# Unread constant products on TensorE ahead of its waits, in a two-layer attention and feed-forward kernel

## The chip, the core and the metric

One Trainium2 chip; the program runs on one of its cores. The metric is the device time of one execution in microseconds (us). Three runs of the kernel before took 1187.93, 1188.32 and 1190.07 us; the median is 1188.32 us.

## The reference

Two transformer layers over 2 batches of 1024 tokens with 256 features. Each layer adds an attention and a feed-forward part, both computed from the same layernorm of x:

```python
xn = _layernorm(x)
x = x + attn0(xn) + ffn0(xn)   # causal, 32 heads of 8 on 8 kv heads, rope; gelu ffn on values rounded to e4m3
xn = _layernorm(x)
x = x + attn1(xn) + ffn1(xn)   # see below
```

`attn1` regroups the tokens by position, with 16 heads of 16. `ffn1` rounds its weights to ternary values per group of 64, multiplies silu(gate) by up, normalises the rows by their root mean square and projects back.

## The kernel before

The tokens lie as 16 tiles `xs` of 128 rows. `xnT` holds the layernorm, transposed, in four chunks of 512 tokens.

**Layer 0** is `attention0`. `project` makes q and k, `split` cuts each into three bfloat16 parts (on VectorE for the first chunk, on GpSimd later), and `load_q` brings the parts back through DRAM into `qmain` and `qlast`. SyncE issues these DMAs in program order. For each of the 16 query tiles i (listed in `order`) there are two passes over the keys. `max_unit` (masks L887, scores L910, tile `m`) feeds the row maximum on VectorE (`mx`, L922); `take_max` and `turn_max` send the maxima through DRAM into `qlast` (L949, L951). `weigh` then makes the shifted scores (L974, tile `s`), ScalarE takes the exponential (L984, `p`), and `gather` multiplies by v (L1004, `acc`). `one_slot` interleaves three streams by counting: the maxima of later tiles (`advance`), the pieces of the layer-0 feed-forward (`ffn0`, tiles `gu`, `f0o`), and the ternary weights and second layernorm. A ternary piece is three steps of VectorE (L329, L331, L332) behind a product (`tpsg`, L327). `next_late` runs pieces of the layernorm of layer 1 for chunks whose sums are ready. `rest_of_weights` and `next_late` are each called from a slot. TensorE's instructions keep the order in which the code records them (`manual_schedule`); the order on VectorE, ScalarE, GpSimd and SyncE is made by a scheduler from estimated times.

PSUM pools in layer 0: `ps_s` (3 buffers, tiles `m` and projections), `ps_t` (4 buffers, nearly all else, `s` and `vp` among them), `ps_acc` (1).

**Layer 1** is `layer1`, whose order is a heap of functions keyed by due times: `at(delay, f)` puts f at `now + delay`. Unit 1.0 of that time is about one `ffn_unit` (`f1gu`, L627). For each chunk: `project` (`pqk` L435, `pv` L452), `turn` (`pt` L464, then a write `qkv` and loads of `qs`, `ks`, `vs` by SyncE, L467 and L469), `scores` (`sq` L484, maximum on VectorE L492, which goes through DRAM into `qs`, L494 and L497), `shifted` (`sk` L519 and the exponential L527), `weighted` (`acc` L534), `normalise` (`ot` L548, VectorE L550 and L552), `turn_back` (`ob` L564, `rows` L565). The last chunk ends in `attended_by_heads` (`ao` L592): 32 products for each of four token groups, 16 rows deep, whose sums VectorE adds to x (L596) before the output DMAs. `ffn_out` is `f1o` (L662).

Of the kernel before, what the change touches and what calls it, by code (L numbers as in the profile page):

```python
# [10 lines left out]
F32 = mybir.dt.float32  # L11
# [8 lines left out]
P = 128  # L20
# [28 lines left out]
def two_layers(ctx: ExitStack, tc: tile.TileContext, a: dict, out: bass.AP):  # L49
    nc = tc.nc  # L50
# [18 lines left out]
    ident_bf = cp.tile([P, P], BF, tag="ident_bf", name="ident_bf")  # L69
# [4 lines left out]
    for name, op, fill, sign in (  # L74
# [5 lines left out]
        for e in range(2):  # L80
            for t in range(2):
                part = m[HALF * e : HALF * e + HALF, t, :]
                nc.gpsimd.affine_select(
                    out=part,
# [8 lines left out]
    groups = cp.tile([P, P], BF, tag="groups", name="groups")  # L93
# [36 lines left out]
    wv1 = k0_flat[0][:, 1024:1536].rearrange("p (k n) -> p k n", k=2)  # L130
    wp = k0_flat[1].rearrange("p (c d) -> p c d", d=D)


    mark = [None]

# [254 lines left out]
    def layer1(w, wgu, wp, cs, sc):  # L390
# [8 lines left out]
        with ExitStack() as es:  # L399
            pool = es.enter_context(tc.tile_pool(name="l1", bufs=2))  # L400
            dram = es.enter_context(tc.tile_pool(name="l1d", bufs=2, space=bass.MemoryType.DRAM))
            ps_s = es.enter_context(tc.tile_pool(name="l1s", bufs=1, space=PSUM))
            ps_gu = es.enter_context(tc.tile_pool(name="l1gu", bufs=2, space=PSUM))
# [8 lines left out]
            for n in range(2):  # L412
                q, k, v = (pool.tile([P, NH, P], F32, tag=f"{x}{n}", name=f"{x}s{n}", bufs=1) for x in "qkv")
                nc.gpsimd.memset(v, 1.0)
                for s in range(4):
                    nc.sync.dma_start(
                        out=k[S * s + HD : S * s + HD + 9], in_=a["same"][0, :, None, :].to_broadcast([9, NH, P])
                    )
                    nc.sync.dma_start(
                        out=q[S * s + HD : S * s + HD + 8], in_=a["same"][1, 0:8, None, :].to_broadcast([8, NH, P])  # L420
# [8 lines left out]
            def project(c, i):  # L429

                x = [xnT[c][:, k, i * P : (i + 1) * P] for k in range(2)]
                nm = f"{c}{i}"
                pqk = ps_m.tile([P, 512], F32, tag="m", name=f"pqk{nm}")
                for k in range(2):
                    nc.tensor.matmul(pqk, x[k], wqk[:, k, :], start=(k == 0), stop=(k == 1))  # L435

                pairs = pqk.rearrange("p (h f e) -> p h f e", f=8, e=2)
                shape = [P, 2 * NH, 2, 8]
                qk = pool.tile(shape, F32, tag="qk", name=f"qk{nm}")
                qk2 = pool.tile(shape, F32, tag="qk2", name=f"qk2_{nm}", bufs=1)  # L440
                for to, e, tab in ((qk, 0, cs), (qk2, 1, sc)):
                    nc.vector.tensor_tensor(
                        to,
                        pairs[:, :, None, :, e].to_broadcast(shape),
                        tab[:, None, :, (4 * c + i) % 8, :].to_broadcast(shape),
                        ALU.mult,
                    )
                nc.gpsimd.tensor_tensor(qk, qk, qk2, ALU.add)
                pv = ps_m.tile([P, 2, P], F32, tag="m", name=f"pv{nm}")
                for u in range(2):  # L450
                    for k in range(2):
                        nc.tensor.matmul(  # L452
                            pv[:, u, :], wv[:, k, u * P : (u + 1) * P], x[k], start=(k == 0), stop=(k == 1)
                        )
                all_t = pool.tile([P, 6, P], F32, tag="all", name=f"all{nm}")
                nc.scalar.copy(all_t[:, 4:6], pv)
                at(0.5, lambda: turn(c, i, qk, all_t))
# [187 lines left out]
            def ffn_scale(n):  # L645
                ss = hidden[n][1]
                pss = ps_m.tile([P, 4], F32, tag="m", name=f"pss{n}")
                for i in range(4):
                    nc.tensor.matmul(pss[:, i : i + 1], ss[:, i * P : (i + 1) * P], ones, start=True, stop=True)
                ms = pool.tile([P, 4], F32, tag="ms", name=f"ms{n}")  # L650
                nc.vector.tensor_scalar(ms, pss, 1.0 / HID, None, ALU.mult)
                inv = rsqrt(pool, ms, 4, RMS_EPS, f"f1_{n}")

                times = (0.1, 0.5, 0.9, 1.3) if n != chunks[-1] else (1.7, 2.85, 3.7, 4.3)
                for i, t in enumerate(times):
                    at(t, lambda i=i: ffn_out(n, i, inv))
# [40 lines left out]
            def at(delay, f):  # L697
                heapq.heappush(queue, (now + delay, next(counter), f))

            counter = itertools.count()  # L700
            for p, c in enumerate(chunks):
                for i in range(4):
                    at(8.0 * (p - 1) + 2.0 * i - 0.4 if p else 0.9 * i - 5.0, lambda c=c, i=i: project(c, i))
                for b in range(4):
                    at(8.0 * p + 2.0 * b, lambda c=c, b=b: scores(c, b))
                for hc in range(NHC):
                    at(8.0 * p + hc - 4.7, lambda c=c, hc=hc: ffn_unit(c, hc))
                at(8.0 * p + 8 - 4.7 + 0.6, lambda c=c: ffn_scale(c))
# [4 lines left out]
            while queue:  # L713
                now, _, f = heapq.heappop(queue)
# [3 lines left out]
    def attention0(w, qlast, tables):  # L718
# [11 lines left out]
        with ExitStack() as es:  # L730
# [3 lines left out]
            ps_s = es.enter_context(tc.tile_pool(name="a0s", bufs=3, space=PSUM))  # L734
            ps_t = es.enter_context(tc.tile_pool(name="a0t", bufs=4, space=PSUM))
# [129 lines left out]
            slot = 0  # L865
# [13 lines left out]
            def add_mask(out, start, stop):  # L879


                for t in range(2):
                    lo = HALF * t
                    for e in range(2):
                        rows = slice(HALF * e, HALF * e + HALF)
                        rhs = mask_q[rows, t, None, lo:]
                        nc.tensor.matmul(  # L887
                            out[e][:, :, lo:],
                            ident_h[rows, t, :],
                            rhs.to_broadcast([HALF, out[e].shape[1], P - lo]),  # L890
                            start=start and t == 0,
                            stop=stop and t == 1,
                        )


            mx = {}
# [219 lines left out]
            }  # L1116
            ready = []
            late, self_end, added = [], object(), [0] * NT
            unit = next(units)
            next(unit)  # L1120

            def rest_of_weights(u):
                with tc.issue_after(reduced.ins):
                    next(u, None)

            def next_weights():

# [15 lines left out]
                        after(6, lambda c=chunks: late.append(layernorm(1, c, pool, ps_t, "t")))  # L1143

            def next_late():
                if next(late[0], self_end) is self_end:
                    late.pop(0)

# [3 lines left out]
            at = 0  # L1152
            credit = share = 0.0
            cost_left = sum(cost for _, cost, _ in maxima)
# [2 lines left out]
            done_at = {}  # L1157

            def advance():
                nonlocal at, credit, cost_left  # L1160
                n, cost, unit = maxima[at]
                ready.extend(extra.pop(n, ()))
                unit()
                if ready:
                    ready.pop(0)()
                at += 1
                credit -= cost
                cost_left -= cost
                if cost == 0:
                    done_at[n] = slot  # L1170
                    if n >= 3:
                        next_weights()

            def one_slot(weights):

                nonlocal credit, share, pairs_left, pieces_left
                rate = max(cost_left / max(pairs_left - TAIL, 1), 512.0) * (1.0 if weights else 1.5)
                credit = min(credit + rate, 2.0 * rate)
                while at < len(maxima) and credit > 0 and order[maxima[at][0]] in qst:
                    advance()  # L1180
                share += max(pieces_left, 0) / max(pairs_left - TAIL, 1)
                if share > 0:
                    share -= 1.0
                    with tc.issue_after(reduced.ins):
                        next(pieces, None)
                    pieces_left -= 1
                if late and slot % 3 == 0:
                    with tc.issue_after(reduced.ins):
                        next_late()
                pairs_left -= weights  # L1190
                tick()

            group, waiting = [], None
            for n, (b, i) in enumerate(order):
                if n and n + 3 < len(order):
                    load_q(*order[n + 3])
                while n not in done_at or slot < done_at[n] + (LEAD if n > 2 else SHORT):
                    one_slot(False)
                for G in range(2):
                    for j in range(i + 1):  # L1200
                        for u in range(2):
                            one_slot(True)
                            if u and waiting:
                                gather(*waiting)
                            group += weigh(b, i, 2 * G + u, j)
                        waiting = (b, i, G, j, group)
                        group = []
# [116 lines left out]
```

## Time and profile before

| what | value |
|---|---|
| profiled execution, device time | 1187.45 us |
| its span (first to last instruction) | 1185.7 us |
| mean granted TensorE clock | 0.921 of full |
| busy: TensorE, VectorE, ScalarE, GpSimd | 86%, 65%, 46%, 28% of the span |
| median of three runs | 1188.32 us |

Line numbers are those of the kernel before. In the slices of the page each digit is a fortieth of the span (29.6 us) in tenths; `PEclk` is the TensorE clock that was granted. In the timeline a row is: start, length, engine, line, operation, output and inputs with their sizes, count, and in brackets the idle time of the engine just before and what ended it. In the waits a row is: who waited, for whom, us in total, times, longest. In the table of stretches a row is: the stretch and its length, then busy us (and instructions) of TensorE products, TensorE weight loads, VectorE, ScalarE, GpSimd, then the granted clock, the DMA share and GB/s.

### The profile page before, as it was taken

What the parts mean: (1) busy time and instruction counts of PE and PEld (TensorE: products, weight loads), DVE (VectorE), ACT (ScalarE), POOL (GpSimd) and SP (SyncE); (2) the same over time, 40 slices, a digit from 0 to 9 for tenths busy, and PEclk for the clock granted to TensorE, in tenths of its full rate; (3) what the DMA queues carried; (4) which work ended last, traced back from release to release, by engine and by line L of the source; (5) the groups of instructions that cost most, each with busy time, mean ns of one, the idle gap of its engine ahead of it and who ended that gap; (6) DMA issues with size and microseconds to landing.
All of it is one profiled execution on the core that took longest, in us unless ns stands there. A gap on an engine that the chain in (4) does not pass through costs nothing.

```text
span 1185.7 us, 19115 instructions
## 1 busy us (share of the span) xinstructions
PE 1021.4 (86%) x7340; PEld 493.4 (42%) x7340; DVE 765.5 (65%) x1448; ACT 542.6 (46%) x981; POOL 336.0 (28%) x384
## 2 busy tenths in 40 slices
PE   5463897897988989897989998978999999999987
PEld 2231331232432222232323333334576676676676
DVE  6677988889688997789896889244323334333321
ACT  1112352673456747576767776732223323323320
POOL 2023223314244021412123326454213313312200
PEclk9586797997899989998999999999899999999986
DMA  6631001002101010100010110029331421521200
GB/s 193 154 105 37 23 1 43 17 21 61 34 14 41 1 27 19 36 1 17 11 27 3 26 27 5 3 27 136 52 48 28 93 52 28 91 46 28 46 11 18
DMA packets 78850, 48.98 MB, mean 41 GB/s; under 512 B 31816, under 2 KB 73800, under 8 KB 78760
## 3 DMA queue, kind: packets, MB, share of 16 engines
q1 hardware_dynamic: 75512, 43.32, 17.5%
q0 software_dynamic: 2960, 4.20, 1.7%
q8 instruction: 57, 0.93, 0.3%
q14 instruction: 33, 0.27, 0.1%
q10 hardware_dynamic: 288, 0.26, 0.1%
HBM read 34.12 MB, written 15.20 MB: 42 GB/s over the span
## 4 chain that ended last, share of the span: by engine, by line
PE 57%; DVE 26%; DMA 4%; ACT 4%; issue 4%; POOL 3%; SPq 2%; DVEq 0%; ACTq 0%; POOLq 0%
DVE mx L922 14%; PE f1gu L627 9%; PE acc L1004 8%; PE s L974 7%; PE f1o L662 5%; PE m L910 3%; PE sk L519 3%; PE sq L484 3%; PE pqk L435 2%; PE gu L283 2%; PE m L887 1%; PE acc L534 1%; ACT p L984 1%; PE ao L592 1%; PE ot L1019 1%
## 5 line engine op out<-in xcount | busy, mean ns | idle before, releaser
L922 DVE TENSOR_REDUCE mx<-m 128x1 f32<-128x512 f32 (+3 forms) x608 | 372.8, 654 | 89.2 <-PE m L910 51.4
L984 ACT ACTIVATE p<-s 128x512 f32<-128x512 f32 x576 | 306.8, 605 | 147.6 <-PE s L974 144.4
L1004 PE MATMUL acc<-p,v 128*9 128x512 f32 x1152 | 171.2, 619 | 1.8 <-ACT p L984 1.2
L910 PE MATMUL m<-k,qmain 64*128 64x512 bf16 (+3 forms) x384 | 93.6, 361 | 53.1 <-DVE mx L922 36.1
L988 POOL TENSOR_SCALAR_AFFINE_SELECT p<-p 128x512 f32<-128x512 f32 x128 | 84.3, 682 | 175.7 <-ACT p L984 175.4
L627 PE MATMUL f1gu<-xnT,wgu 128*128 128x512 f32 x256 | 118.4, 606 | 1.6 <-DVE wgu L1229 1.6
L910 PE MATMUL m<-kmain,qmain 64*128 64x512 bf16 (+3 forms) x384 | 83.1, 332 | 24.5 <-DVE mx L922 22.6
L910 PEld LDWEIGHTS <-qmain 64*128 64x128 bf16 x768 | 50.2, 99 | 88.4 <-issue 62.9
L641 POOL TENSOR_TENSOR sq<-h 128x512 f32<-128x512 f32 x28 | 29.1, 1039 | 182.3 <-DVE h L637 182.3
L887 PEld LDWEIGHTS <-ident_h 64*128 64x128 bf16 x832 | 45.0, 97 | 84.0 <-issue 60.9
L974 PE MATMUL s<-qlast,k 35*128 35x512 bf16 x288 | 65.3, 399 | 16.4 <-DMA qlast<-mscr 16.4
L887 PE MATMUL m<-mask_q,ident_h 64*128 64x128 bf16 (+3 forms) x832 | 74.2, 221 | 3.2 <-DVE mx L922 2.2
L974 PE MATMUL s<-qmain,k 64*128 64x512 bf16 x288 | 69.0, 401 | 8.8 <-DVE att L1027 3.0
L627 PEld LDWEIGHTS f1gu<-xnT,wgu 128*128 128x128 f32 x256 | 47.6, 196 | 51.2 <-issue 47.9
L974 PEld LDWEIGHTS <-k 64*128 64x128 bf16 (+1 forms) x576 | 21.3, 96 | 114.4 <-issue 105.9
L974 PE MATMUL s<-qmain,kmain 64*128 64x512 bf16 x288 | 64.0, 389 | 4.8 <-ACT p L984 2.2
L636 DVE SCALAR_TENSOR_TENSOR h<-h,f1gu 128x512 f32<-128x512 f32 x32 | 21.9, 686 | 65.6 <-ACT h L635 65.6
L662 PE MATMUL f1o<-k,h 128*128 128x256 f32 x256 | 61.7, 398 | 0.5 <-DVE on L552 0.4
L974 PE MATMUL s<-qlast,klast 35*128 35x512 bf16 x288 | 61.1, 386 | 0.0
L492 DVE TENSOR_REDUCE m<-sq 128x16 f32<-128x2048 f32 x16 | 36.7, 2292 | 34.6 <-PE sq L484 33.9
L662 PEld LDWEIGHTS f1o<-k,h 128*128 128x128 f32 x256 | 50.5, 200 | 9.7 <-issue 1.7
L635 ACT ACTIVATE h<-f1gu 128x512 f32<-128x512 f32 x32 | 19.1, 597 | 64.6 <-PE f1gu L627 64.6
(270 smaller groups left out, 1556.5 us busy)
## 6 DMA issues: line engine op xcount, KB each, us to landing
qmain<-qscr SPq DMA_DIRECT2D x64, 96.0 KB
qkv<-all SPq DMA_DIRECT2D x16, 384.0 KB
qscr<-ptq SPq DMA_DIRECT2D x32, 96.0 KB
x<-in_x SPq DMA_DIRECT2D x16, 128.0 KB
qmain<-qscr SPq DMA_DIRECT2D x32, 64.0 KB
qs<-qkv SPq DMA_DIRECT2D x16, 128.0 KB
ks<-qkv SPq DMA_DIRECT2D x16, 128.0 KB
vs<-qkv SPq DMA_DIRECT2D x16, 128.0 KB
```

Source lines behind the costliest of these rows:

```text
L484: nc.tensor.matmul(ps[:, s, r, :], columns(q, slice(S * s, S * s + HD + 8), 4 * b + r), columns(k, slice(S * s, S * s + HD + 8), 4 * b + r ...
L492: nc.vector.tensor_reduce(m, ps, AX.X, ALU.max, negate=True)
L519: nc.tensor.matmul(ps[:, s, r, :], columns(k, slice(S * s, S * s + HD + 9), 4 * b + r), columns(q, slice(S * s, S * s + HD + 9), 4 * b + r ...
L627: nc.tensor.matmul(ps[g], wgu[:, k, g * HID + hc * P : g * HID + (hc + 1) * P], xnT[n][:, k, :], start=(k == 0), stop=(k == 1),)
L662: nc.tensor.matmul(po, hs[hc // 2][:, hc % 2, i * P : (i + 1) * P], wp[:, hc, :], start=(hc == 0), stop=(hc == NHC - 1),)
L887: nc.tensor.matmul(out[e][:, :, lo:], ident_h[rows, t, :], rhs.to_broadcast([HALF, out[e].shape[1], P - lo]), start=start and t == 0, stop ...
L910: nc.tensor.matmul(sc[e][:, s * width : (s + 1) * width], qst[b, i][0][rows, p, :], kst[b][0][rows, p // 4, lo : lo + width], start=not fo ...
L922: reduced = nc.vector.tensor_reduce(mx[b, i][:, part, e, pairs[0] : pairs[0] + n], sc[e][:, : n * width].rearrange("p (s k) -> p s k", s=n ...
L974: nc.tensor.matmul(sc[e], kst[b][n][rows, u, j * P : (j + 1) * P], qst[b, i][n][rows, 4 * u : 4 * u + 4, :], start=n == 0, stop=n == 1,)
L984: nc.scalar.activation(p, sc[e], AF.Exp, scale=scale)
L988: nc.gpsimd.affine_select(out=by_head, in_=by_head, compare_op=ALU.is_ge, fill=0.0, base=0, pattern=[[0, 4], [1, P]], channel_multiplier=-1,)
L1004: nc.tensor.matmul(acc[32 * s : 32 * s + HD0 + 1, :], vst[b][:, j, 4 * G + s, :], ps[s], start=(j == 0), stop=(j == i),)
```

## The change

A helper issues n products of two constants (`groups` as stationary, the identity repeated four times as moving operand: 128 rows, 512 columns, bfloat16) into a PSUM tile that nobody reads. It is called in these places; nothing else is edited.

```diff
+    def keep_busy(out, n):
+        rhs = ident_bf[:, None, :].to_broadcast([P, 4, P])
+        for _ in range(n):
+            nc.tensor.matmul(out.rearrange("p (h q) -> p h q", h=4), groups, rhs, start=True, stop=True)
...
+            def busy_later(delay, pool_, n):
+                def f():
+                    tag = "gu" if pool_ is ps_gu else "s"
+                    shape = [P, 512] if pool_ is ps_gu else [P, 4, 512]
+                    t = pool_.tile(shape, F32, tag=tag, name=f"busy1_{next(counter)}")
+                    keep_busy(t if pool_ is ps_gu else t[:, 0], n)
+                at(delay, f)
...
+            for t, n in ((-4.51, 11), (-1.81, 7), (-0.01, 10)):
+                busy_later(t, ps_s, n)
+            for t, n in ((25.99, 8), (27.99, 8), (29.49, 5), (32.9, 4), (33.36, 4)):
+                busy_later(t, ps_gu, n)
...
+            def wait_busy(n):
+                if n:
+                    keep_busy(ps_t.tile([P, 512], F32, tag="t", name=f"busy{slot}_{n}"), n)
...
             def rest_of_weights(u):
+                nonlocal long_steps
                 with tc.issue_after(reduced.ins):
                     next(u, None)
+                long_steps += 5
...
             def next_late():
+                nonlocal long_steps
+                long_steps += 2
...
             def advance():
...
+                if at == 0:
+                    wait_busy(56)
+                wait_busy(long_steps)
+                long_steps = 0
                 unit()
...
+                if n == 0:
+                    wait_busy(50)
                 for G in range(2):
```

Counted in the built program, that is 247 products: 56 ahead of the first `max_unit`, 50 ahead of the first `weigh`, 84 in 24 blocks of layer 0 (60 behind the 12 ternary pieces, 24 behind 12 layernorm pieces; each ahead of the next `max_unit`, one ahead of a later `ao`), 28 in three blocks at the start of layer 1 and 29 in five blocks at its end. In layer 0 the tile of a block takes the next of the four `ps_t` buffers.

The scheduler reorders a few instructions of the other engines around this. Two of the moves are not neighbours' swaps. On VectorE, two maxima (`mx`, L922) and a conversion step (`wg`, L198 and L200) go from ahead of the layernorm statistics of chunks 2 and 3 (L160) to behind its reciprocal root. At the start of layer 1, the second pair of `qk` (L442) goes behind the four `xn` steps (L172) of the last layernorm, and on ScalarE the first copy `all` (L465) behind the square root (L145).

More of the change, by code (lines that the diff above doesn't have):

```diff
@@ L1159, in advance @@
             def advance():
-                nonlocal at, credit, cost_left
+                nonlocal at, credit, cost_left, long_steps
                 n, cost, unit = maxima[at]
                 ready.extend(extra.pop(n, ()))
+                if at == 0:
+                    wait_busy(56)
+                wait_busy(long_steps)
+                long_steps = 0
                 unit()
```

## The prediction

> **What bounds the kernel now.** I read the page's slices first, then its chain of waits, then TensorE's waits, then the table of stretches over every time at which the granted clock was 0.5.
>
> ```profile
> PE   5463897897988989897989998978999999999987
> DVE  6677988889688997789896889244323334333321
> PEclk9586797997899989998999999999899999999986
> ...
> PE 57%; DVE 26%; DMA 4%; ACT 4%; issue 4%; POOL 3%; SPq 2%; DVEq 0%; ACTq 0%; POOLq 0%
> ```
>
> TensorE holds 57% of the chain and VectorE 26%: in layer 0 (to 785 us) the two alternate, in layer 1 TensorE rules alone. The clock row is the point of the change: it dips where TensorE had waited. One product of exactly the added shape stands in the timeline, at both clocks:
>
> ```profile
> 230.23 1.89 PE L283 MATMUL gu<-xq,wg 128*128 128x512 bf16 x4
> ...
> 558.18 1.04 PE L283 MATMUL gu<-xq,wg 128*128 128x512 bf16 x4
> ```
>
> Four products, the last ending 0.61 and 0.39 us after its start, so one step costs (1.89-0.61)/3 = **0.427 us at half clock** and (1.04-0.39)/3 = **0.217 us at full**. Weight loads ran beside these. Nearest rows bound a step from both sides: a pair of 64-row products in 0.22 us (0.11 each) below, 0.427 above; I take 0.217 and 0.427.
>
> The stretches at half clock add up to 188 us from 21 us on, with TensorE busy for some 138 us of them. If all of that were TensorE-bound, half of it, 69 us, would be the price; most is not, because VectorE is the bound there.
>
> The Trainium skill (TensorE: Matmul & The Clock Gate, Part 1) says that the warm-up penalty is under 1% of a typical kernel's span and not worth modelling. By it the whole change could bring at most 12 us. The 138 us above don't bear that out as a limit, and no term below uses it.
>
> **Part 1, 56 products ahead of the first maxima.** TensorE idles 12.74 us from 32.8 to 45.5 for the q load. But the block's PSUM tile takes the buffer of the first `vp`, and the built program makes it wait for the first `v` addition (timeline):
>
> ```profile
> 37.10 0.61 DVE L860 TENSOR_TENSOR v<-vp,bv_bc 128x64 f32<-128x64 f32 x4
> ...
> 47.46 0.58 PE L910 MATMUL m<-k,qmain 64*128 64x128 bf16 x7 [1.71 <-DMA qlast<-qscr]
> ```
>
> So it starts at 37.3, when the clock has already fallen (35.0). The clock rose 4.2 and 3.1 us after dense work began at 10.4 and 21.7; the steps of the clock lie 3.41 us apart, so here at 41.9. 4.6 us at 0.427 are 10.8 products, the other 45.2 take 9.8 us: end 51.7. Masks and the first scores need 0.7, so the first maximum starts at 52.4 instead of 48.0: 4.4 late. Being warm gives back 3 x 0.4 (each unit of 1.9 us has 0.62 of VectorE waiting for TensorE), 0.9 (`lnt` 1.97 to 1.1) and 1.4 (`k01p` 5.0 to 3.64). **+1.0 us**; a rise at 3.1 or 6.8 us makes it +0.3 or +2.1.
>
> **Part 2, 50 products ahead of the first `weigh`.** TensorE waits there from 87.6 to 104.0, its longest wait:
>
> ```profile
> PE s L974 <- DMA qlast<-mscr: 16.4, 1, 16.4
> ```
>
> and in the table of stretches this one, at half clock throughout, is the longest:
>
> ```profile
> 79.40:110.10 30.70, 11.09 (x87) 6.06 (x89) 22.70 (x55) 6.07 (x11) 5.34 (x7) 0.50 0.11 28
> ```
>
> The block starts at about 86, runs cold to 89.6 (9 products) or 93.1 (16), and ends by 98.5 to 100.6: before the wait does. What sets that wait is not TensorE: ScalarE holds the cast of q (94.53) behind a square root (94.42) that needs eight statistics from VectorE (89.85 on), and SyncE holds `mscr` behind that q. The move on VectorE takes two maxima (0.55 each), 1.22 and 0.43 out from ahead of the statistics, less overlap: **-2.45 us**. It costs that these now wait for the block, where VectorE otherwise idles from 99 to 105. Then the work from 104.0 to 110.1 runs warm: `acc` 1.70 to 1.05 and three slots of scores by 0.4, partly covered by VectorE: **-1.5** (0 to -2.5).
>
> **Part 3, 24 blocks in layer 0, 84 x 0.217 = 18.2 us of TensorE.** From 170 to 760 us TensorE waits for the maxima and VectorE waits for scores about as much (TensorE's waits):
>
> ```profile
> PE m L910 <- DVE mx L922: 58.6, 93, 2.8
> ```
>
> I went through the timeline at each block. Free, since TensorE idles for VectorE just behind: at 175.0 (idle 2.60), 221.3 (2.10), 274.0 (1.23, for ScalarE), 476.8 (1.35), 531.9, 537.7, 560.6, 649.8 (1.03), 728.8. Paid in part: 348.5, 716.4 (0.5 each), 542.6 with 545.6 (0.3), 570.4 (0.2), 735.1 (0.3). Paid: 415.5 and 602.2 (1.1 each: VectorE was waiting for these scores), 684.2 (0.6), 525.3, 566.2, 740.9 and the one ahead of `ao` (0.43 each), 556.7 (0.3). Sum 6.6. What they save: the half-clock stretches at 229.6 (behind the idle 2.10; 1.0) and 550.4 (behind an idle of 2.81; VectorE waits 1.09 in it; 1.2). The long ones, from 181.8, 284.2 and 424.2, begin 5 to 10 us behind their blocks and stay. **+4.4 us**; ends -2.2 (all free) and +18.2 (nothing free, nothing saved). That most of a block lies on idle time is the row nearest to it, so I keep to the low half.
>
> **Part 4, the start of layer 1.** The blocks of 11, 7 and 10 take 2.4, 1.5 and 2.2 us in idle gaps of 2.57, 1.90 and 2.90. The first makes `pqk` 1.5 us faster, and that is worth nothing: SyncE issues the first `qkv` write only at 800.78, and DMA sets the pace to 830.5. The moved `qk` may delay the second tile by up to 1.0; I take 0, since it ends near where it was. The third block counts:
>
> ```profile
> 833.41 5.47 PE L627 MATMUL f1gu<-xnT,wgu 128*128 128x512 f32 x8
> ...
> 839.16 3.60 PE L627 MATMUL f1gu<-xnT,wgu 128*128 128x512 f32 x8
> ```
>
> 5.47 to 3.60 and `pt` 1.11 to 0.60: **-2.4 us**, and TensorE is the bound from there on.
>
> **Part 5, the end.** Two blocks of 8 (1.7 us) in idle gaps of 2.05 and 2.06 ahead of `sq`, where a half-clock window follows each:
>
> ```profile
> 1093.73 1.93 PE L534 MATMUL acc<-p,vts 128*32 128x128 f32 x32
> 1095.60 4.17 PE L627 MATMUL f1gu<-xnT,wgu 128*128 128x512 f32 x8
> ...
> 1160.24 1.08 PE L534 MATMUL acc<-p,vts 128*32 128x128 f32 x32
> ```
>
> 0.85 + 0.57 + 0.1 (`sq`) = 1.5 each: **-3.0**. The block of 5 (1.1) in the gap of 1.56 ahead of the `sk` at 1132.35: `sk` 3.3 to 2.1 and `f1o` 5.88 to 3.72: **-3.3**, if the window then passes. The two blocks of 4 (0.87 each) fill gaps of 0.81 and 0.68, at about +0.2, and `ao` starts warm:
>
> ```profile
> 1168.30:1171.70 3.40, 3.40 (x36) 2.98 (x32) 0.00 (x0) 0.00 (x0) 0.00 (x0) 0.50 0.00 0
> 1171.70:1175.10 3.40, 3.40 (x36) 2.97 (x32) 0.00 (x0) 0.00 (x0) 0.00 (x0) 0.50 0.00 0
> ```
>
> TensorE is busy throughout and the clock does not rise: products 16 rows deep don't lift it. So I expect it to fall after one warm window. `ao` is 32 steps of four, 0.427 cold (13.7 in all); one step warm, as for `f1o` of the same 256 columns, is 0.217. With 3.4 us warm instead of 0.75, 2.6 less, net **-2.4**; ends 0 and -5.8 (warm to its end). Behind `ao` only the additions and the output remain, so it comes off the time whole.
>
> The same page (table "Why this matters for your kernels") asks for no idle gap over about 3 us. Here the clock fell behind gaps of 1.56 and 2.05 us. By the page parts 4 and 5 would be worth nothing, and the sum would be 1189 us.
>
> **Sum:** +1.0 - 2.45 - 1.5 + 4.4 - 2.4 - 3.0 - 3.3 - 2.4 = -9.65. Against the profiled execution (1187.45; span 1185.7 and 1.75 around it) that is 1177.8; the median of the runs is 0.9 higher, so **1178.0 us**.
>
> **Rivals.** About 0.2% (2.4 us) can be told from no change.
> - *The layer-0 blocks hide wholly and `ao` stays warm*: part 3 -2.2, `ao` -5.8: 1187.45 - 19.65, **1168**. For: nine blocks lie on idle time already. Against: VectorE waits for scores at 415.5 and 602.2.
> - *The clock falls all the same*: a window that is half filled may count as idle (0.51 to 0.56 busy fell at 1130.7 and 130.6). Then part 1 +1.0, part 2 -2.45, part 3 +4.4, one block of 8 and the third of layer 1 -3.9: **1186.5**, no change.
> - *TensorE is the bound in layer 0* (the other side): the 84 products of part 3 fall on the path at 0.217 each, +18.2, where the rest brings -14.05: **1191.6**, slower. It decides once over 14 of the 18.2 us are paid. For: VectorE waits there for `m` as long as TensorE waits for it, and each block takes one of four `ps_t` buffers, so the next `weigh` may wait for an exponential. Against: 69 us of TensorE's time from 170 to 760 are idle (520.7 busy of 590).
>
> **Chances.** Forecast 0.52 (own range 1172 to 1184), first rival 0.20, second 0.12, third 0.16. Faster by over 0.2%: 0.72; within: 0.12; slower: 0.16. The range takes the first three, 1167 to 1189; most of the third is left out.
>
> **What would show it.** Part 1: first maximum later than 48.0 by about 4 us. Part 2: the first `s` of `qlast` near 102.5, full clock behind it. Part 3: idle of TensorE before `m` shrinking by 10 us or more; if VectorE's wait for `m` grows as much, the third rival. Part 4: no half clock ahead of 840. Part 5: `ao` in 10 to 11 us with its first part at 0.217. The forecast is wrong if the half-clock stretches from 830 on are still there, or if 170 to 760 us became longer by over 10 us.

## The result and the profile after

The changed kernel takes **1201.76 us** (median of 4 runs, 1199.76 to 1203.36) beside 1188.98 before: ratio 1.0111, 95% interval 1.0089 to 1.0133. It is slower by 13 us; 1178 was forecast. Its profiled execution has a span of 1200.8, 15.1 more than before.

The slices of the page after, and its chain:

```profile
PE   5777797997998989898989999989999999999998
...
PEclk8878897998997989999999999999999999999889
...
PE 62%; DVE 25%; ACT 4%; DMA 3%; POOL 2%; issue 2%; SPq 1%; DVEq 0%; ACTq 0%; POOLq 0%
```

The granted clock is higher (0.934 in the mean, 0.921 before; the second slice went from 5 to 8, the last from 6 to 9), and yet the time is longer: TensorE's share of the chain grew from 57% to 62%. So the change does to the clock what it says, and loses elsewhere.

Where: I matched TensorE's products of the two traces one by one. The lag is how much later a product starts than the same one before.

| stretch (us of before) | forecast | lag gained after |
|---|---|---|
| to the first `weigh`, 104 (56 and 50 products) | -1.45 | +1.9 |
| 104 to 124 | -1.5 | -0.3 |
| 124 to 773 (blocks of layer 0) | +4.4 | **+20.6** |
| 773 to 860 (start of layer 1) | -2.4 | -0.8 |
| 860 to 1090 | 0 | -3.1 |
| 1090 to 1118 (one block of 8) | -3.0 with the other 8 | -1.7 |
| 1118 to 1166 (the other 8, the 5) | -3.3 | +4.6 |
| `ao` to the end | -2.4 | -6.1 |
| sum | -9.65 | +15.1 |

The -3.1 lies where the change adds nothing; 2.5 of it is the clock: the half-clock stretch of before at 1018 to 1021 has none to answer it in this execution.

Both engines' waits, TensorE's first (changed kernel), then VectorE's (changed kernel, then before):

```profile
PE m L936 <- DVE mx L948: 55.0, 89, 2.6
...
PE s L1000 <- DMA qlast<-mscr: 2.4, 1, 2.4
```

```profile
DVE mx L948 <- PE m L936: 71.9, 49, 11.0
```

```profile
DVE mx L922 <- PE m L910: 51.4, 43, 6.1
```

The wait ahead of the first `weigh` went from 16.4 to 2.4, and the long stretch at half clock around it broke up (table of stretches, changed kernel):

```profile
83.40:93.70 10.30, 7.12 (x49) 3.84 (x49) 9.70 (x24) 0.00 (x0) 0.00 (x0) 0.50 0.15 41
93.70:107.30 13.60, 10.78 (x60) 4.81 (x59) 8.44 (x26) 3.60 (x6) 2.62 (x3) 1.00 0.14 34
107.30:114.10 6.80, 6.43 (x36) 2.00 (x37) 6.45 (x11) 2.75 (x7) 3.79 (x6) 0.50 0.03 7
```

But TensorE's wait for the maxima shrank only from 58.6 to 55.0, while VectorE's wait for scores grew by 20.5 (16.3 of it among the blocks, from 170 to 760 us of before; the rest at the first maximum). As the sign of its third rival the forecast had named a TensorE wait shorter by 10 us or more and a VectorE wait longer by as much; only the second half of that is here. From 173.4 to 782.2 (170 to 760 before) TensorE is busy 545.1 of 608.8 us (520.7 of 590): its idle time shrank by 5.6, its busy time grew by 24.4.

### The profile page after: what moved, and what is told of

The parts are those of the page before. It is cut to its first block, busy times and chain, and to the rows that moved or that the text cites. A ratio compares the mean times of both kernels' runs of the same rounds, so it can differ in the third digit from the quotient of the medians.

```text
span 1200.8 us, 19591 instructions
## 1 busy us (share of the span) xinstructions
PE 1073.8 (89%) x7571; PEld 507.9 (42%) x7587; DVE 762.4 (63%) x1448; ACT 544.9 (45%) x981; POOL 334.6 (28%) x384
## 4 chain that ended last, share of the span: by engine, by line
PE 62%; DVE 25%; ACT 4%; DMA 3%; POOL 2%; issue 2%; SPq 1%; DVEq 0%; ACTq 0%; POOLq 0%
DVE mx L948 14%; PE f1gu L634 9%; PE acc L1030 8%; PE s L1000 7%; PE f1o L669 5%; PE busy L139 4%; PE m L936 4%; PE sk L526 3%; PE sq L491 3%; PE gu L290 2%; PE pqk L442 2%; PE m L909 2%; ACT p L1010 2%; PE acc L541 1%; PE ao L609 1%
## 5 line engine op out<-in xcount | busy, mean ns | idle before, releaser
L936 PEld LDWEIGHTS <-qmain 64*128 64x128 bf16 x768 | 47.5, 98 | 82.6 <-issue 60.0
L909 PE MATMUL m<-mask_q,ident_h 64*128 64x128 bf16 (+3 forms) x832 | 71.5, 218 | 2.3 <-DVE mx L948 2.1
L139 PE MATMUL busy<-ident_bf,groups 128*128 128x512 bf16 x247 | 65.1, 409 | 7.8 <-DVE v L882 6.2
```

The source lines that it names most:

```text
L139: nc.tensor.matmul(out.rearrange("p (h q) -> p h q", h=4), groups, rhs, start=True, stop=True)
L909: nc.tensor.matmul(out[e][:, :, lo:], ident_h[rows, t, :], rhs.to_broadcast([HALF, out[e].shape[1], P - lo]), start=start and t == 0, stop ...
L936: nc.tensor.matmul(sc[e][:, s * width : (s + 1) * width], qst[b, i][0][rows, p, :], kst[b][0][rows, p // 4, lo : lo + width], start=not fo ...
```

## The experiments

All kernels below are the changed kernel with fewer or moved blocks. A diff with `-` lines is against it; one with `+` lines alone is against the kernel before, with the change's helpers left in. "ao" is the closing group of 16-row products, "layer 0" the start of layer 1's first product (`pqk`); both are from the one profiled execution, the rest from all runs. Ratios are to runs of the kernel before on the same chip (medians there 1187.8 to 1189.4).

| run | products kept | median us | ratio (95%) | layer 0 | ao |
|---|---|---|---|---|---|
| before | none | 1188.98 | | 784.9 | 13.4 |
| changed | all | 1201.76 | 1.0111 (1.0089 to 1.0133) | 807.1 | 7.2 |
| e1_blocks | layer-0 blocks | 1195.57 | 1.0062 (1.0038 to 1.0087) | 800.9 | 7.2 |
| e2_no_blocks | all but layer-0 blocks | 1185.36 | 0.9978 (0.9956 to 1.0) | 785.9 | 7.2 |
| e3_layer1 | eight blocks of layer 1 | 1182.42 | 0.9951 (0.9931 to 0.9972) | 788.3 | 7.2 |
| e4_ahead_weigh | the 50 | 1177.43 | 0.9905 (0.9872 to 0.9939) | 785.2 | 7.2 |
| s4_dense | 4 elsewhere | 1188.52 | 0.9998 (0.997 to 1.0027) | 785.2 | 7.2 |
| s10_dense | 10 elsewhere | 1188.21 | 1.0006 (0.9975 to 1.0037) | 789.2 | 13.3 |
| f24_single | layer-0 blocks of one | 1181.16 | 0.9949 (0.9926 to 0.9972) | 790.6 | 7.2 |
| f_one_at_348 | one layer-0 block | 1189.94 | 1.0017 (0.9991 to 1.0043) | 790.8 | 13.3 |
| h1_ao | 4 + 4 ahead of ao | 1182.34 | 0.9966 (0.9945 to 0.9987) | 788.1 | 7.2 |
| h2_weigh_ao | 50, 4 + 4 | 1175.07 | 0.9888 (0.9857 to 0.9918) | 785.4 | 7.2 |
| h3_blocks_ao | layer-0 blocks, 4 + 4 | 1195.38 | 1.0053 (1.0031 to 1.0075) | 804.5 | 7.2 |
| h4_first_ao | 56, 4 + 4 | 1180.33 | 0.9935 (0.9909 to 0.9961) | 787.9 | 7.2 |
| k1_without_two | layer-0 blocks but two, 4 + 4 | 1186.07 | 0.9979 (0.9961 to 0.9997) | 796.9 | 7.2 |
| k2_behind_scores | layer-0 blocks behind scores, 4 + 4 | 1186.45 | 0.9974 (0.9953 to 0.9996) | 796.7 | 7.2 |
| k3_first_weigh_ao | 56, 50, 4 + 4 | 1185.21 | 0.9947 (0.9928 to 0.9966) | 789.5 | 7.2 |
| k4_weigh_start_ao | 50, 11 + 7 + 10, 4 + 4 | 1176.37 | 0.9895 (0.9873 to 0.9917) | 787.0 | 7.2 |
| l1_27_weigh_ao | 27, 50, 4 + 4 | 1175.63 | 0.9903 (0.9866 to 0.9939) | 784.6 | 7.2 |
| k5_weigh_end | 50, 8 + 8 + 5 + 4 + 4 | 1179.69 | 0.9933 (0.9907 to 0.9959) | 784.9 | 7.2 |

One execution differs from the next by several us here: where the code of layer 0 is untouched, it ends between 784.9 and 789.2 in five traces.

### Which part loses: e1_blocks, e2_no_blocks, e3_layer1, e4_ahead_weigh

e1_blocks drops these lines:

```diff
-            for t, n in ((-4.51, 11), (-1.81, 7), (-0.01, 10)):
-            for t, n in ((25.99, 8), (27.99, 8), (29.49, 5), (32.9, 4), (33.36, 4)):
...
-                    wait_busy(56)
...
-                    wait_busy(50)
```

e2_no_blocks drops `wait_busy(long_steps)` alone, e3_layer1 all three `wait_busy` calls, and e4_ahead_weigh all but `wait_busy(50)`.

> Only the 24 blocks of layer 0 (84 products). The forecast's part 3 says +4.4, so 1193.4 beside 1189.0 before. Theory A (each product falls on the path: between 124 and 773 us the changed kernel's TensorE fell behind by 20.6 us): +18 to +23, 1207 to 1212. Theory B (the blocks hide and the changed kernel loses elsewhere): under +8.

> Everything but the 24 blocks of layer 0. The forecast's other parts say -14.05, 1175. Theory A with the lags read off the changed kernel's trace (+1.6 behind parts 1 and 2, about -7 over layer 1): 1183 to 1184, faster than before. Theory B (the loss isn't in the blocks): no faster than before.

> Only the eight blocks of layer 1. Forecast: -2.4 at the start and -8.7 at the end, 1178. By the lags of the changed kernel's trace: start -0.8, second block of 8 +3.9 (it landed ahead of a score product that waits for nothing), the rest of the end -9, about 1183. If the changed kernel's gains in layer 1 are only what a later start gives anyway: 1187 to 1189.

> Only the 50 products ahead of the first weighing. Forecast: -2.45 for VectorE's order and -1.5 for the clock, 1185. By the lag of the changed kernel (-2.2 at the first score of the weighing, -0.3 behind it): 1186.5. If what is won there is waited for again within layer 0 (VectorE's maxima set the pace): within 1 of before.

e1 fell just inside theory B's range (+7.4 us by the ratio, under 8 expected), e2 gained a mere 2.6, between its two theories, and e4 brought more than any of its expectations (-11.3). They don't add up: e1 and e2 make +5, the whole change +13. The traces say why e1 looks cheap. Its layer 0 ends 16.0 later than before's (800.9), and its layer 1, the same code as before, takes 392.9 where before's profiled execution took 400.7. Most of that is `ao`: 7.2 us at full clock in place of 13.4. So a warm `ao` is counted in e1 and in e2.

### Is it only where the clock's grid falls: s4_dense, s10_dense

```diff
+            for t, n in ((6.2, 4),):     # ((6.2, 10),) in s10_dense
+                busy_later(t, ps_gu, n)
```

No other block is kept.

> None of the change's blocks; instead 4 products (0.87 us) in the middle of layer 1's dense work at 874 us, where TensorE waits for nothing. In the profile of before the clock fell at 1018, 1093, 1110, 1154 and 1168 us; in that of the 50 products alone, with the same code in layer 1, not at 1018 and 1168. Theory C (which windows of 3.41 us are half empty is decided by where the work lies on the clock's grid, and the grid lies alike in most runs): a shift of 0.87 moves them, and the time falls by 3 to 8, to 1181 to 1186. If the grid lies differently in every run: +0.9.

> The same with 10 products (2.17 us). Theory C: a shift of 2.17 puts the work on the grid about where the run with the 50 products alone had it: faster than before by 3 to 9 although only work was added. If the grid lies differently in every run: +2.2, 1190.8.

Both are the same as before. Theory C falls. The clock changes only at points 3.41 us apart, its grid, and the grid starts anywhere: in the 20 traces the changes of the clock lie 0.2 to 3.4 us (modulo 3.41) behind the first product. What its place gives or takes is spread over the runs of one kernel (1179.1 to 1193.1 for s4) and doesn't shift the median. The Trainium skill (TensorE: Matmul & The Clock Gate, Part 1) says the same of the window, that it runs freely and one kernel differs by it from run to run; the traces agree.

### Products or places: f24_single, f_one_at_348

Both keep blocks of layer 0 alone, as e1_blocks does:

```diff
-                wait_busy(long_steps)
+                wait_busy(min(long_steps, 1))                                     # f24_single
+                keep_n += 1 if long_steps else 0                                  # f_one_at_348
+                wait_busy(long_steps if keep_n == 4 and long_steps else 0)        # f_one_at_348
```

> The 24 blocks of layer 0 with one product each (5.2 us in place of 18.2); the order on GpSimd changes in fewer places and no longer at 348 us. The 24 blocks alone cost 6.9. If their products' time counts: 6.9 x 5.2 / 18.2 = 2, 1190.6. If the place, the PSUM buffer and the order on the other engines count: +5 to +7. The forecast's working would give at most +1.

> Of the 24 blocks only the one at 348 us (5 products, 1.1 us), which alone puts two of GpSimd's additions of the feed-forward (x, L256) behind the last two steps of a ternary piece. The 24 blocks' trace falls behind by 4.9 there, that of the whole change by 6.8, with TensorE waiting 2.4 for ScalarE's cast and half clock for 13.7 us behind it. If that order is the cause: +4 to +7 at 380 us, and +3 to +7 on the time. If the product time is: +0.5 to +1.1.

f24_single came out 6 us faster than before, outside both expectations: its `ao` ran warm, and 11 of its 12 runs are below 1186. Why its `ao` starts warm so much oftener than before's is not shown. In layer 0 its trace lies 10.3 before that of e1, for 13.2 us of products less (61 at 0.217). f_one_at_348 can't be told from before by its time (+2.0, -1.1 to +5.1); its trace shows the mechanism. GpSimd (f_one_at_348, then before):

```profile
356.54 1.16 POOL L343 TENSOR_TENSOR wgu_bf<-tmg,twg 128x512 bf16<-128x512 bf16 x1
357.65 0.67 POOL L263 TENSOR_TENSOR x<-x,ob 128x256 f32<-128x256 f32 x1
358.27 0.59 POOL L328 DMA_DIRECT2D twg<-in_w_gate_up  x1
358.88 0.68 POOL L263 TENSOR_TENSOR x<-x,ob 128x256 f32<-128x256 f32 x1
```

```profile
354.05 0.67 POOL L256 TENSOR_TENSOR x<-x,ob 128x256 f32<-128x256 f32 x1
354.68 1.15 POOL L335 TENSOR_TENSOR tmg<-tmg,twg 128x512 bf16<-128x512 bf16 x1
355.79 0.67 POOL L256 TENSOR_TENSOR x<-x,ob 128x256 f32<-128x256 f32 x1
356.42 1.15 POOL L336 TENSOR_TENSOR wgu_bf<-tmg,twg 128x512 bf16<-128x512 bf16 x1
```

The same run's ScalarE and TensorE:

```profile
359.60 0.37 ACT L259 CAST ob<-f0o 128x256 bf16<-128x256 f32 x1 [3.85 <-POOL x L263]
```

```profile
360.31 0.37 PE L996 MATMUL s<-qmain,k 64*128 64x512 bf16 x1 [2.43 <-ACT ob L260]
```

The two additions now stand behind all four steps of the ternary piece. They hold the buffers of `ob`, so ScalarE's cast waits for them, the exponentials behind it wait too, and TensorE gets no free PSUM buffer for 2.43 us. Five unread products of 1.1 us moved an order on GpSimd, and its trace stands 3.5 behind at 360 us and 4.6 at 410, of which 1.1 were there ahead of the block. With one product there (f24_single) the additions keep their old places, and the lag stays at 1.3 across it.

### With ao made certain: h1_ao, h2_weigh_ao, h3_blocks_ao, h4_first_ao

To compare the other parts, all of these have the two blocks of 4:

```diff
+            for t, n in ((32.9, 4), (33.36, 4)):      # all four
...
+                    wait_busy(56)                     # h4_first_ao
+                wait_busy(long_steps)                 # h3_blocks_ao
...
+                    wait_busy(50)                     # h2_weigh_ao
```

> Only the two blocks of 4 around the last transpose, ahead of the closing ao. In the traces so far ao takes either 7.2 us (full clock to its end) or 13.3 to 13.4 (half), never between, and the runs of before cluster near 1181 and near 1189. Theory D (products 16 rows deep keep the clock they begin with, and before begins them at half clock in about four runs of five): all runs in the lower cluster, 1180 to 1186, median 5 below before. The forecast's term -2.4 (warm for one window only): 1186.5, with ao 10 to 11 us.

> The 50 products ahead of the first weighing and the two blocks of 4. With ao warm in both, this less the blocks of 4 alone is what the 50 are worth by themselves: by the trace of the 50 alone -1 to -3 at the end of layer 0. If that run's -11.2 was ao beginning warm by chance for the most: 1176 to 1180 here. If the 50 bring 11 by themselves: 1172.

> The 24 blocks of layer 0 and the two blocks of 4. Theory A (the products of the blocks fall on the path): this less the blocks of 4 alone is 14 to 19, so 1197 to 1203, and the +6.9 of the 24 blocks alone was that less an ao that began warm. If the blocks cost 7: 1190.

> The 56 products ahead of the first maxima and the two blocks of 4. The forecast's part 1: +1.0 on the blocks of 4 alone. The trace of the whole change: 4.8 late at the first score and 4.1 at 69 us, so +2 to +4 if nothing takes it up later; 0 if VectorE's later waits do.

Theory D held: h1's twelve runs lie in 1181.6 to 1187.7 (one above the 1186 expected), before's in 1180.9 to 1193.1, and `ao` takes 7.2. The table of stretches in the changed kernel, the two that are all `ao`:

```profile
1189.40:1192.80 3.40, 3.40 (x70) 3.23 (x68) 0.00 (x0) 0.00 (x0) 0.00 (x0) 1.00 0.02 5
1192.80:1196.20 3.40, 3.30 (x64) 2.75 (x56) 0.03 (x1) 0.00 (x0) 0.00 (x0) 1.00 0.00 0
```

TensorE is as busy as in the stretches of before shown above, with the same products, and the clock stays at 1.00 for good. On that base the 50 bring another 7.3 us, the 56 another 2.0 (their intervals overlap), and the layer-0 blocks cost 13.0, all by the medians (by the ratios 9.3, 3.7 and 10.3).

### Where a block stands: k1_without_two, k2_behind_scores

Lag by block, h3 against h1 up to the next block: between -1.4 and 1.2 at eighteen of the blocks, 1.8 and 2.5 at two, but 5.4 at the block of 348 and 3.6 at the one of 7. (The 84 products stand in 23 tiles, not 24: one holds a ternary and a layernorm piece, 7 products.) k1 is h3 without these two, k2 is h3 with every block behind the scores that it stood ahead of:

```diff
-                wait_busy(long_steps)
+                wait_busy(0 if keep_n == 4 or long_steps == 7 else long_steps)     # k1_without_two
...
                 unit()
+                wait_busy(long_steps)                                              # k2_behind_scores
```

> The blocks of layer 0 without two of them (the 5 products at 348 us and the 7 at 735 us), and the two blocks of 4 ahead of ao. Beside the run with all blocks and the 4s (13.0 above the 4s alone, 1195.4): its trace falls behind by 5.4 at the first of the two (GpSimd's order, then half clock) and by 3.6 at the second (the block itself waits 1.5 for a PSUM buffer that an exponential holds, ahead of scores that waited for nothing). Theory E (these two places make most of the cost): 3 to 7 above the 4s alone, 1185.5 to 1189.5. Theory A (84 products at one price, 72 left): 13.0 x 72 / 84 = 11, 1193.5.

> All blocks of layer 0 and the two blocks of 4, but each block of layer 0 behind the masks and scores that it stood ahead of, so that VectorE's maxima are not held up by it. Theory A (TensorE's own time is the bound): the same 1195 as ahead of them. Theory F (what costs is that a block stands between a waiting VectorE and its scores, or waits for a PSUM buffer there): at most 8 above the 4s alone, under 1191.

k1 is 3.7 above h1, k2 4.1 (by the ratios 1.5 and 1.0): of the 13.0, two blocks make some 9, and the same 84 products cost under a third of it from behind the scores. So theory A, TensorE's time as the bound, falls; E and F hold. The traces put it less strongly: at the end of layer 0, h3 lies 16.4 behind h1, k1 8.8 and k2 8.6, and then layer 1, with the same code, takes 387.1 to 388.6 us in these three and 392.3 in h1; why is not shown. In k2's trace it is the same two blocks that still cost: 5.5 at 348, where GpSimd's additions stand behind the four steps as before and TensorE waits 2.52 for the cast, and 2.8 at the block of 7, which waits 0.94 for its buffer. All the others cost 0.2 there together, in place of some 7.5 in h3: the place behind the scores mends those, not the two. The block of 7 in the changed kernel, on TensorE and then on VectorE:

```profile
752.72 0.58 PE L1000 MATMUL s<-qlast,klast 35*128 35x512 bf16 x2
754.80 2.16 PE L139 MATMUL busy<-ident_bf,groups 128*128 128x512 bf16 x7 [1.49 <-ACT p L1010]
756.89 0.82 PE L909 MATMUL m<-mask_q,ident_h 64*128 64x512 bf16 x4
```

```profile
758.17 1.29 DVE L948 TENSOR_REDUCE mx<-m 128x4 f32<-128x512 f32 x2 [2.66 <-PE m L936]
```

and the same place in e2_no_blocks, without it:

```profile
735.83 0.58 PE L1000 MATMUL s<-qlast,klast 35*128 35x512 bf16 x2
736.06 0.58 PE L909 MATMUL m<-mask_q,ident_h 64*128 64x512 bf16 x3
```

There the masks and scores follow the `s` products at once, since they write another pool. In the changed kernel the block stands between, and its tile needs a `ps_t` buffer that an exponential still reads, held up by a table load of 1.28 us. It waits 1.49, the clock falls at 755.8, 1.0 into the block, its products take 2.16, and only then come the scores, for which VectorE has waited 2.66.

### The 56, and the rest of layer 1: k3_first_weigh_ao, k4_weigh_start_ao, l1_27_weigh_ao, k5_weigh_end

```diff
+            for t, n in ((-4.51, 11), (-1.81, 7), (-0.01, 10)):                             # k4
+            for t, n in ((32.9, 4), (33.36, 4)):                                            # k3, k4, l1
+            for t, n in ((25.99, 8), (27.99, 8), (29.49, 5), (32.9, 4), (33.36, 4)):        # k5
...
+                    wait_busy(56)                                                           # k3
+                    wait_busy(27)                                                           # l1
...
+                    wait_busy(50)                                                           # all four
```

> The 56, the 50 and the two blocks of 4. Alone with the 4s, the 50 brought 7.3 more and the 56 brought 2.0 more. The change without the layer-0 blocks brought only 3.3 in all. If the 56 and the 50 hinder each other (the 56 push the work up to the 50's wait back by 4.8): no better than the 50 with the 4s, 1175 to 1179. If they add up: 1173. If neither, and the six other blocks of layer 1 lost the rest: 1173 to 1176.

> The 50, the three blocks at the start of layer 1 and the two blocks of 4. Forecast's part 4: -2.4 on the 50 with the 4s (1175.1), 1172.7. By the whole change's trace (TensorE 2.5 later at 796, 0.8 earlier at 860 than at 785): -0.8, 1174. If these blocks are what the change without the layer-0 blocks lost: above 1178.

> As the run with the 56, the 50 and the two blocks of 4, with 27 in place of 56. At 0.427 us to the clock's rise near 41.9 and 0.217 behind it, 27 end at about 45.5, when q's last part arrives; 56 end 6 later. Theory (the 56 hurt beside the 50 because their excess makes the first scores 4.8 late, and what precedes the 50's wait with them): first scores no later than 46.5, and with the 50 and the 4s 1172 to 1176, as without any first block or up to 3 better. If a full clock there is what hurts, whatever its length: 1181 to 1185, as with 56.

> The 50 and all five blocks at the end of layer 1 (8, 8, 5, 4, 4). Beside the 50 with the 4s alone (1175.1): the forecast's terms for the 8s and the 5 say -6.3, 1169. By the order of the built program the second 8 stands ahead of a score product of the last tile that waits for nothing (1.7 for its products, and 2 or more if half clock follows, as in the trace of the whole change), the first 8 in the gap of 2.06 (-1.5), the 5 in that of 1.56 (0 to -1): 1176 to 1178.

Beside the 50 the 56 lose 10 us by the medians (7 by the ratios), more than expected; 27 lose nothing that can be told. In the changed kernel, and in l1_27_weigh_ao:

```profile
37.32 14.77 PE L139 MATMUL busy<-ident_bf,groups 128*128 128x512 bf16 x56 [6.21 <-DVE v L882]
52.02 0.50 PE L909 MATMUL m<-mask_q,ident_h 64*128 64x512 bf16 x4
```

```profile
38.00 7.80 PE L139 MATMUL busy<-ident_bf,groups 128*128 128x512 bf16 x27 [5.69 <-DVE v L880]
45.73 0.50 PE L907 MATMUL m<-mask_q,ident_h 64*128 64x512 bf16 x4
46.07 0.22 PE L934 MATMUL m<-k,qmain 64*128 64x128 bf16 x1
```

Beside the 50 it is the excess over the wait that costs: the first masks come at 52.0 in the one, at 45.7 in the other. How 4.8 us of lateness become 10 is not settled: k3's trace lies 4.1 behind h2's at its end of layer 0, and 6.6 more in layer 1, whose code is the same. The three blocks at the start of layer 1 change nothing (k4 beside h2: 0.9895 and 0.9888), nor did the half clock there go (changed kernel):

```profile
855.19 5.12 PE L634 MATMUL f1gu<-xnT,wgu 128*128 128x512 f32 x8
860.14 0.61 PE L515 MATMUL vt<-ident,vs 128*128 128x128 f32 x4
860.59 3.60 PE L634 MATMUL f1gu<-xnT,wgu 128*128 128x512 f32 x8
```

The 5.47 of before is 5.12, not the 3.60 that I had counted on. The 10 products did fill their gap; but the stretch behind it, 851.4 to 854.8, is busy for 3.07 of its 3.40 us, 2.86 of them with `sq` (24 rows), and the clock fell at its end. The 8, 8 and 5 lose 4.6 by the medians (5.3 by the ratios), more than the built order had let me expect; the second 8, in the changed kernel:

```profile
1138.62 2.07 PE L609 MATMUL ao<-wo,turned 128*128 128x256 f32 x4
1140.49 1.71 PE L656 MATMUL pss<-ones,ss 128*128 128x1 f32 x8
1142.06 2.05 PE L609 MATMUL ao<-wo,turned 128*128 128x256 f32 x4
1143.90 2.42 PE L139 MATMUL busy<-ident_bf,groups 128*128 128x512 bf16 x8
1146.25 2.11 PE L491 MATMUL sq<-ks,qs 24*128 24x128 f32 x32
```

No idle time stands ahead of this `sq`, and before (1122.64 to 1125.7) none did. The block is in the way, with 2.42. The 5 bring next to nothing either: the `sk` behind them takes 3.85 (4.27 before), since its weight loads still wait for `qs` three times, and behind a stretch that it fills to 3.02 of 3.40 us the clock falls at 1158.6, on `f1o`.

## Why the prediction was wrong, point by point

- **The sum**: its last step is wrong by itself, since 1177.8 and 0.9 make 1178.7 (and part 1's terms make +0.9). Of the 23 us (by the ratios) between the forecast of -9.65 and the result, part 3 makes 11.4 (the changed kernel against e2: 15.8 for 4.4), and the other parts the same (e2: -2.6 for -14.05).
- **The price of a product** was right: the 56 took 14.77, 14.4 had been worked out, and the first scores came 4.8 late for 4.4.
- **Part 1, what it gives back**: 3.5 was expected of a warm TensorE behind the block, 0.7 had come by 69 us. The clock fell again at 56.1; a warm start isn't kept through work with VectorE's gaps. Alone with the 4s the 56 do no harm (h4); beside the 50 they cost 7 to 10 in place of +1.0.
- **Part 2**: the first `s` came 3.2 (e4) and 2.5 (h2) earlier, -2.45 had been worked out. The -1.5 for the clock isn't seen: full from 93.7, it falls at 107.3 (changed kernel), as soon as VectorE sets the pace again (from 103.9 to 107.3 TensorE is busy for 0.93 us, VectorE throughout). The time of e4 and h2 falls by more than the lag of layer 0 explains (785.2 and 785.4 beside 784.9 to 789.2 untouched), through a layer 1 of 389.2 and 388.6 us in place of 392.3 (h1), with the same code. What passes that on stays open; single traces of this code with a warm `ao` lie anywhere from 387.1 to 395.2.
- **Part 3 is the single step that failed most**: +4.4 forecast, 13.0 measured by h3 against h1 (10.3 by the ratios), 16.4 by the changed kernel against e2 (15.8). Most blocks cost what was written down: 415 us 1.2 for 1.1, 542 to 550 a gain of 1.0 for one of 0.9, 477 nothing. Two that were put at nothing, at 274.0 and 649.8, took 1.8 and 2.5 (in k1 0.4 and 1.0). Two failed by far. The block at 348.5, put at 0.5, became 5.4, because I took the moves on GpSimd for neighbours' swaps that cost nothing and did not follow who waits for the moved additions. The one at 735.1, put at 0.3, became 3.6, because I counted a product's time where the block had to wait for its own buffer, 1.49 us in the changed kernel. I had written of the four `ps_t` buffers, but for the `weigh` behind a block, not for the block.
- **Part 4**: two half-clock windows became one (854.8 to 858.2), but it lies on the same products, and k4 shows no gain. The step that failed is that a filled gap keeps the clock up; here it fell behind the few-row `sq`.
- **Part 5** failed three times: for the 8s and the 5, -6.3 had been worked out, and k5 measured +4.6 (5.3 by the ratios). The two 8s were put at the gaps of 2.05 and 2.06; in the built order they stand ahead of the second of these and of a `sq` without a gap, so one gap (2.05 at 1109.96 in the changed kernel) stays and one block is pure cost. The -3.3 of the 5 took `sk` to be held by the clock (3.3 to 2.1), and full clock took only 0.4 off it. For `ao`, -2.4 was too little: 16-row products don't lift the clock, as written, but they don't let it fall either, so `ao` keeps the clock that it begins with, worth 6.2 in one execution and 5.5 in the median (h1), as some executions of before begin warm of themselves.
- **The signs**: both that were to show the forecast wrong came. From 170 to 760 us became 18.8 longer (608.8 for 590), and half clock is still there behind 830.
- **The Trainium skill's "under 1%"** (TensorE: Matmul & The Clock Gate, Part 1) is said of the ramp over the first products, not of every later fall of the clock, so the 12 us that I worked out of it bound nothing here.
- **The rivals**: the third gave the direction; of its sign in the waits VectorE's half came, TensorE's (4 us among the blocks for 10) did not, and its cause was another. Were TensorE's time the bound, k2 would be as slow as h3. The first rival's warm `ao` came true together with it.

The best of these kernels is h2_weigh_ao, the 50 and the two blocks of 4: ratio 0.9888 (0.9857 to 0.9918), 13 us faster than before and 27 faster than the change. l1 and k4, with more products, lie within its interval.

## What to carry to other kernels

Filler for TensorE's clock paid here where TensorE was known to wait, for not much more than the wait (the 4s, of 1.03 us, in gaps of 0.81 and 0.68), with a buffer that was free at once; where one of these three failed, it turned into a wait of its own. Where another engine waits for TensorE's products, it should stand behind them, not ahead (k2). And a scheduler that orders the other engines sees the filler too: every instruction that it moves is part of the price, and each must be followed to who waits for it.

## What the runs showed of the hardware

- The clock seems to have two bounds; the figures are a fit to these traces. Over 20 traces, of 5705 stretches of 3.41 us at full clock 440 were followed by half clock; "TensorE busy below 0.6 of the stretch" tells all but 143 of them rightly (of the falls it misses about a quarter). Of 937 at half clock 440 rose; "busy above 0.91" tells all but 69. Between the two the clock mostly stays as it was.
- Products with few rows count for less than their busy time. Of the full-clock stretches over 90% busy from 35 us on, none of 3574 was followed by half clock where products of at most 25 rows made up to 60% of the busy time, and 31 of 467 were where they made more. `ao` (16 rows) took 7.2 or 13.3 to 13.4 us in all 20 traces, never between. And in the kernel before this stretch was full, mostly of `sk` (25 rows), and half clock followed it:

```profile
1151.20:1154.60 3.40, 3.40 (x36) 2.90 (x35) 0.48 (x1) 0.58 (x1) 0.00 (x0) 1.00 0.05 2
1154.60:1158.00 3.40, 3.40 (x17) 2.64 (x10) 0.00 (x0) 1.88 (x1) 0.00 (x0) 0.50 0.00 0
```

- So gaps far below 3 us decide. The Trainium skill (TensorE: Matmul & The Clock Gate, "Why this matters for your kernels") asks for no gap over about 3 us; here 8 products in gaps of 0.81 and 0.68 were worth 5.5 us (h1).
